# Four layers of gated attention: layer 2's norms and centred values placed inside layer 1's last steps, and its position products in a written TensorE order

## The chip, the cores and the metric

The kernel runs on one core of a Trainium2 chip. Its time is the device time of one execution in microseconds (us). A core has five engines with a queue of instructions each, which run side by side and wait for one another through semaphores: TensorE (PE in the profile, with PEld for its weight loads), VectorE (DVE), ScalarE (ACT), GpSimd (POOL) and SyncE (SP), which here only issues DMA transfers. TensorE's matrix products go into PSUM, eight banks of 128 by 512 floats; all else is in SBUF, 128 partitions wide.

## The reference

The input x has 16 blocks of 128 tokens by 128 features, and so has the context. Four layers each add two things to x, scaled by the tanh of a gate: a cross-attention on the context, and a feed-forward part, both on a normalised x. The change is at the seam between layer 1 and layer 2.

```python
# layer 1's feed-forward part: 8 components for each output feature, the one with the largest logit is taken
logits = (einsum('bsi,ki->bsk', x, sel_w) + sel_b).reshape(b, s, o, n)
probs = softmax(logits, axis=-1)
hard = one_hot(argmax(probs, axis=-1), n)
mask = stop_gradient(hard - probs) + probs
comp_outputs = einsum('bsi,noi->bsno', x, comp_w) + comp_b[None, None]
output = einsum('bsno,bson->bso', comp_outputs, mask)

# layer 2's attention: q = layernorm(x), k = v = ctx; 8 heads of 16 features
pos_emb = rpe[hops]                               # hops: 128 x 128 indices
ig, fg = gate_in @ igate_w.T + igate_b, gate_in @ fgate_w.T + fgate_b
csum = cumsum(log_sigmoid(fg))                    # with a zero ahead
log_D = csum_row - csum_col + ig, -inf above the diagonal
D = exp(log_D - max(log_D, axis=-1))
k_hop = einsum('bhvc,vmhc->bhvm', qh, pe)         # pe: pos_emb by heads
qk = einsum('bhsd,bhtd->bhst', qh, k / 4)
C = (qk + k_hop) * D
normalizer = maximum(abs(sum(C, axis=-1)), exp(-max_log_D))
h = C / (normalizer + 1e-6) @ vh
hn = layernorm over each head's 16 features, then * (1 + ln_w) + ln_b
```

## The kernel before, in words

All 16 blocks stay in SBUF. They are worked on in four chunks of four blocks (`NJ = 4`, `BJ = 4`, 512 tokens a chunk). `k.x` holds x, `k.xnT` the normalised x with the features on the partitions, `k.ctxT` the context in the same way, and `k.pe` the 128 by 128 position embeddings, gathered during the earlier layers.

**Who decides the order.** The program is written step by step, and a scheduler then puts the instructions of each engine into a fixed queue, by its own estimate of their times and by their dependencies. Where a part of the program sets `k.nc = Engines(...)` (line 47), each of four engines is wrapped in `InOrder` (line 28), which makes every instruction on it follow the one written before: there the written order is the queue's order, for all four engines. `Engines` is in force in layer 1's feed-forward part from line 936 to line 989, and not in layer 2's attention. The profile gives all instructions recorded through `InOrder` the line 38.

**Buffers.** `k.ps(...)` gives one of the PSUM banks. `w2k` is a pool of 13 tiles of 128 by 512, used for the exponentials `l1f_e`, the normalised `xn`, and layer 2's `l2_cm`. `l2_qz` has three buffers, so that queries are made two steps ahead of the products that use them. `l2_vx` lies in the buffer that `l1f_odd` had.

**Layer 1's feed-forward part** (`l1_ffn`, line 841) loops over steps `s`. Chunk `j` has eight components `c`, from 7 down to 0, at the steps 8j to 8j+7: TensorE computes its logits, ScalarE evicts them (`evicted`), VectorE keeps the running maximum `l1f_top` (`largest`). In the eight steps after that, for the same chunk, `less` subtracts the maximum on GpSimd (for the last chunk VectorE takes every odd component), `exped` takes the exponential on ScalarE, `outputs` is the product for the component, ScalarE adds its bias, `chosen` copies by predicate on VectorE, `paired` adds exponentials on GpSimd, and `summed` adds them up on TensorE. Then follow, in halves of 256 columns, `inverted` (the reciprocal into `l1f_r`, VectorE), `finished` (two VectorE operations, `l1f_r` and `l1f_y`), `output` (TensorE turns `l1f_y`) and `added` (VectorE adds it to x). Two tiles take turns for the shifted logits, `l1f_odd` and a part of `k.pe`, so the profile shows the last chunk's subtractions as `pe<-pe,l1f_top`. Chunk 3 finishes all eight pieces in one step, s = 35.

**Norms inside that loop.** `norms` (line 938) lists at which step the norm of which chunk begins. The first three entries are for this part itself, the last three are layer 2's first norm of chunks 0, 1 and 2. Each comes in three pieces, at the step listed, three steps later and five steps later: statistics on VectorE and a power of -1/2 on GpSimd (`ln_st`, `ln_mv`, `ln_rs`); the normalised `xn`, for layer 2's norms by GpSimd; four transposes on TensorE and a copy into `k.xnT`. That copy goes to ScalarE and VectorE in turn (`copy`, line 103). Chunk 3 is normed after the loop (line 990), with `xn` by VectorE.

**Layer 2's attention** (`l2_xattn`, line 1029). `centre` is the matrix that takes each head's mean off. `centred(j)` (line 1061) makes the values of four blocks: four products and a copy by ScalarE into `l2_vx`. `gates` (line 1074) is a generator that makes the gates: the products `l2_gw`, the logarithm of the sigmoid over many small VectorE operations down to `l2_lf`, a cumulative sum as a product (`l2_cs`), a transpose to `l2_gT`, a running maximum `l2_gm` (a scan), and a DMA of it to DRAM. `queries(n)` (line 1130) makes the masked queries of eight positions, four from the front (c = 0, VectorE) and four from the back (c = 1, GpSimd). `hops(n)` (line 1140) multiplies them with the position embeddings, eight products of 128 by 128, and ScalarE copies the results back over `k.pe` (line 1150). `last` does position 127, `biased` adds a bias to x on GpSimd (line 1165). Queries, hops and the steps of the gates alternate in one loop over 16 values of n:

```python
    for n in range(P // 8):
        if n + 2 < P // 8:
            ready[n + 2] = queries(n + 2)
        hops(n, ready.pop(n))
        next(chain, None)
        if n % 4 == 1:
            centred(n // 4)
        if n % 4 == 2:
            biased(n // 4)
```

After it a pipeline over pairs of blocks runs `decays` (line 1184: SyncE brings the maxima back from DRAM as `l2_cm`, GpSimd masks above the diagonal with `affine_select`, ScalarE takes four exponentials of 128 by 128 a tile, line 1203), `masked` (queries of two blocks, `l2_q`, GpSimd), `scores` (line 1216: products, the position scores added by VectorE or TensorE, multiplied with the decays), `values`, `turned`, `normed` (with a power on GpSimd, line 1269) and `added`. The scores need the whole of `k.pe` copied back.

Of the kernel before, what the change touches and what calls it, by code (L numbers as in the profile page):

```python
# [8 lines left out]
F32 = mybir.dt.float32  # L9
# [6 lines left out]
ALU = mybir.AluOpType  # L16
AX = mybir.AxisListType

P = 128
NB = 16  # L20
NJ = 4
BJ = NB // NJ
# [41 lines left out]
class Kernel:  # L64
# [32 lines left out]
    def sq(self, name, dtype=F32):  # L97
        return self.small.tile([P, P], dtype, tag="sq", name=name, bufs=14)
# [95 lines left out]
            except StopIteration as done:  # L194
                return done.value

    def norm(self, j, keep=None, twice=False, pow=None, by=None):

        nc = self.nc
        st = self.sm([P, BJ, 6], "ln_st")
        mv = self.sm([P, BJ, 2], "ln_mv")
        for i in range(BJ):
            nc.vector.bn_stats(st[:, i, :], self.x[:, BJ * j + i, :])
            nc.vector.bn_aggr(mv[:, i, :], st[:, i, :])
        rs = self.sm([P, BJ], "ln_rs")
        if pow is None:
            self.rsqrt(rs, mv[:, :, 1], 1e-5)
        else:  # L210
            nc.vector.tensor_scalar(rs, mv[:, :, 1], 1e-5, None, ALU.add)
            nc.gpsimd.tensor_tensor(rs, rs, pow, ALU.pow)
        yield
        xn = keep if keep is not None else self.w2k("xn").rearrange("p (b d) -> p b d", b=BJ)
        for i in range(BJ):
            (by or nc.vector).tensor_scalar(
                xn[:, i, :], self.x[:, BJ * j + i, :], mv[:, i, 0:1], rs[:, i : i + 1], ALU.subtract, ALU.mult
            )
        yield
        pt = self.ps("tr")  # L220
        for i in range(BJ):
            self.transpose(pt[:, i * P : (i + 1) * P], xn[:, i, :])
        if twice:
            nc.scalar.activation(self.chunk(self.xnT, j), pt, AF.Copy, scale=2.0)
        else:
            self.copy(self.chunk(self.xnT, j), pt)
        return xn

    def normed_rows(self, j, half):
# [48 lines left out]
def bc(ap, shape):  # L278
    return ap.to_broadcast(list(shape))
# [561 lines left out]
def l1_ffn(k):  # L841
# [4 lines left out]
    nc = k.nc  # L846
    C = 8
# [87 lines left out]

    k.nc = nc = Engines(k.tc, k.nc)

    norms = [(0, 1), (6, 2), (12, 3), (33, 0), (37, 1), (41, 2)]
    pieces = {}
    for first, j in norms:  # L940
        for at in (first, first + 3, first + 5):
# [1 line left out]
    under_way = {}  # L943
# [3 lines left out]
    for s in range(C * NJ + 24):  # L947
        j, c = s // C, C - 1 - s % C
# [35 lines left out]
            turn_positions(k, s // 2 + 6)  # L984
        for n in pieces.get(s, []):
            if n not in under_way:
                under_way[n] = k.norm(n[1], pow=k.half, by=nc.gpsimd if n[0] > C * NJ else None)
            next(under_way[n], None)
    k.nc = nc.nc
    k.layernorm(NJ - 1, pow=k.half)  # L990

# [32 lines left out]
    k.nc.scalar.activation(at.rearrange("p v d -> p (v d)"), pt[:, :width], AF.Copy, scale=4.0)  # L1026


def l2_xattn(k):


# [6 lines left out]
    nc = k.nc  # L1038
    H, DH, G = 8, 16, 4
# [6 lines left out]
    own = k.positions.tile([P, 2], F32, name="l2_own")  # L1046
    nc.vector.tensor_reduce(own, k.hm16x8.rearrange("p (g h) -> p h g", h=2), AX.X, ALU.add)
    nc.vector.tensor_scalar(own, own, 0.25, None, ALU.mult)

    centre = k.sq("l2_centre")  # L1050
    nc.vector.tensor_scalar(
        centre.rearrange("p (h d) -> p h d", h=H), bc(k.hm16x8.unsqueeze(2), [P, H, DH]), -1.0 / DH, None, ALU.mult
    )
    nc.vector.tensor_add(centre, centre, k.ident)


    vx = k.wts.tile([P, NB, H, 32], F32, tag="w16b", name="l2_vx")
    nc.gpsimd.memset(vx[:, :, :, DH:], 0.0)
    nc.gpsimd.memset(vx[:, :, :, DH : DH + 1], 1.0)

    def centred(j):
        pv = k.ps("acc")
        for i in range(BJ):
            k.mm(pv[:, i * P : (i + 1) * P], k.ctxT[:, BJ * j + i, :], centre)
        nc.scalar.copy(
            vx[:, BJ * j : BJ * (j + 1), :, 0:DH].rearrange("p b h d -> p (b h) d"),
            pv.rearrange("p (n d) -> p n d", d=DH),
        )

    sq = k.sq  # L1070
    g, low = sq("l2_g"), sq("l2_low")
    gm_d = k.dram.tile([P, P], F32, name="l2_gm_d")
# [1 line left out]
    def gates():  # L1074
# [24 lines left out]
        nc.vector.tensor_mul(u, u, e)  # L1099
        nc.vector.scalar_tensor_tensor(lf, lf, 0.0, u, ALU.min, ALU.subtract)  # L1100

        cs = sq("l2_cs")
        pc = k.ps("acc")[:, :P]
        k.mm(pc, k.tri, lf)
        yield
        nc.vector.tensor_copy(cs, pc)
        nc.vector.tensor_sub(g, ig, cs)
        pt = k.ps("tr")[:, :P]
        k.transpose(pt, g)
        yield  # L1110
# [1 line left out]
        nc.vector.tensor_copy(gT, pt)  # L1112
        nc.vector.tensor_tensor_scan(gm, gT, gT, -3e38, ALU.max, ALU.max)
        nc.sync.dma_start(out=gm_d, in_=gm)

        pt = k.ps("tr")[:, :P]
        k.transpose(pt, gm)
# [12 lines left out]
    def queries(n):  # L1130

        q = k.work.tile([P, 2, 4, H, NB], F32, tag="w4k", name="l2_qz", bufs=3)
        for c, v in enumerate((4 * n, 123 - 4 * n)):
            (nc.gpsimd if c else nc.vector).tensor_tensor(  # L1134
                q[:, c], bc(by_v[:, v : v + 4, :].unsqueeze(2), [P, 4, H, NB]),
                bc(quarter.unsqueeze(1).unsqueeze(3), [P, 4, H, NB]), ALU.mult,
            )
        return q
# [24 lines left out]
    def biased(j):  # L1163
        x = k.x[:, BJ * j : BJ * (j + 1), :]
        nc.gpsimd.tensor_tensor(x, x, bc(lnb.unsqueeze(1), [P, BJ, P]), ALU.add)

    chain = gates()
    ready = {0: queries(0), 1: queries(1)}
    for n in range(P // 8):
        if n + 2 < P // 8:  # L1170
            ready[n + 2] = queries(n + 2)
        hops(n, ready.pop(n))
        next(chain, None)
        if n % 4 == 1:
            centred(n // 4)
        if n % 4 == 2:
            biased(n // 4)
    last()
    next(chain, None)


    by_n = lambda t: t.rearrange("p (b h v) -> p (b h) v", b=2, h=2)
# [769 lines left out]
```

## Time and profile before

| | |
|---|---|
| median of 3 runs | 853.1 us (852.34 to 853.78) |
| profiled execution | 851.53 us |
| its span | 849.8 us |
| TensorE clock granted, mean | 0.919 |
| PE busy | 685.2 us, 81% of the span |
| PEld busy | 469.3 us, 55% |
| DVE busy | 520.3 us, 61% |
| ACT busy | 395.7 us, 47% |
| POOL busy | 452.2 us, 53% |

The span is from the first to the last recorded instruction; the profiled execution took 1.73 us more than its span. The names of the engines and of the views are the profile's. A row of a timeline gives the start and the length in us, the engine, the line, the operation, output and inputs with their shapes, how many instructions follow on one another (x4), and in brackets how long the engine was idle before and what released it. The length of such a group is from its first start to its last end. The chain of waits follows the work that ended last back from the end, at each step to what released it. Matmuls of floats come as two passes each, so 16 rows are eight products. Numbers behind tile names and digits in them are left out by the profile (`l_qz` is `l2_qz`).

### The profile page before, as it was taken

How to read it: one execution, taken by the hardware profiler on the slowest of the kernel's cores; microseconds unless marked ns; L12 is line 12 of the kernel's file. 1: busy time of each engine (PE TensorE's matmuls, PEld its weight loads, DVE VectorE, ACT ScalarE, POOL GpSimd, SP SyncE). 2: the span in 40 equal slices, each digit the busy share in tenths (PEclk: the TensorE clock that was granted, in tenths of full speed). 3: DMA queues.
4: the chain of work that ended last, by engine and by line, in shares of the span. 5: the costliest groups of instructions: out<-in, count | busy, mean ns of one | idle time of the engine just before them, and what ended most of it. 6: DMA issues, size and time to landing. Idle time of an engine off the chain costs nothing.

```text
span 849.8 us, 13272 instructions
## 1 busy us (share of the span) xinstructions
PE 685.2 (81%) x4321; PEld 469.3 (55%) x4321; DVE 520.3 (61%) x1463; ACT 395.7 (47%) x1001; POOL 452.2 (53%) x482
## 2 busy tenths in 40 slices
PE   3169993677897999899848798956999878999997
PEld 3159993343453555443328743434788765655556
DVE  5825553674645555788977456986411765777862
ACT  0025550442543455686505937511744355666552
POOL 5666656733744774686875916862200334555420
PEclk9999996787998999899959989875999999999999
DMA  8557773110000000000030405230000000000001
GB/s 262 133 172 212 207 175 91 49 35 10 20 13 20 23 24 23 3 0 1 2 98 20 146 1 161 77 124 15 11 1 0 1 2 1 1 0 1 1 7 43
DMA packets 43652, 46.47 MB, mean 55 GB/s; under 512 B 8368, under 2 KB 32560, under 8 KB 43456
## 3 DMA queue, kind: packets, MB, share of 16 engines
q1 hardware_dynamic: 37088, 35.63, 14.3%
q0 software_dynamic: 4384, 8.95, 4.3%
q10 hardware_dynamic: 2112, 1.05, 0.4%
q8 instruction: 34, 0.56, 0.3%
q14 instruction: 34, 0.28, 0.1%
HBM read 40.90 MB, written 4.72 MB: 54 GB/s over the span
## 4 chain that ended last, share of the span: by engine, by line
PE 50%; DVE 22%; issue 7%; POOL 7%; ACT 6%; DMA 3%; DVEq 0%; POOLq 0%; SPq 0%; ACTq 0%
PE ps_bank L112 21%; PE ps_bank L38 16%; PE ps_mm L112 4%; PE ps_acc L112 4%; DMA l_back<-l_out_d,l_rows 2%; ACT l_cm L1203 2%; DVE l_m L38 2%; DVE l1f_r L38 2%; PE ps_bank L116 1%; POOL l_ss L1269 1%; PE ps_mm L38 1%; DVE xn L38 1%; ACT pe L1150 1%; DVE xnT L38 1%; DVE l_up L38 1%
## 5 line engine op out<-in xcount | busy, mean ns | idle before, releaser
L1009 POOL DMA_INDIRECT pe<-in_L_xattn_rpe,itokT x65 | 64.6, 994 | 65.9 <-DVE l_top L739 20.9
L38 PE MATMUL ps_bank<-xnT,l1f_w 128*128 128x512 f32 x128 | 62.5, 618 | 0.4 <-ACT pe L38 0.4
L739 DVE TENSOR_REDUCE l_top<-ps_bank 128x8 f32<-128x512 f32 x64 | 39.8, 684 | 30.3 <-PE ps_bank L112 30.3
L486 DVE TENSOR_SCALAR l_h<-ps_mm,l_w 128x128 f32<-128x128 f32 x117 | 33.8, 345 | 35.4 <-ACT l_h L488 34.1
L771 ACT ACTIVATE l_a<-ps_bank 128x512 f32<-128x512 f32 x64 | 33.2, 602 | 45.8 <-PE ps_bank L112 45.7
L456 POOL DMA_INDIRECT l_xs<-l_rows_d,l_tok x39 | 37.0, 949 | 24.2 <-PE ps_acc L112 14.3
L112 PE MATMUL ps_acc<-l_w,l_h 128*128 128x128 f32 x312 | 45.5, 279 | 1.5 <-DVE l_y L498 1.3
L1203 ACT ACTIVATE l_cm<-l_cm,l_g 128x128 f32<-128x128 f32 x128 | 40.2, 404 | 13.9 <-POOL l_cm L1196 13.9
L112 PE MATMUL ps_mm<-l_xT,l_w 128*128 128x128 f32 x312 | 44.2, 279 | 0.4 <-ACT l_xT L471 0.4
L112 PEld LDWEIGHTS ps_acc<-l_w,l_h 128*128 128x128 f32 x312 | 40.0, 193 | 2.4 <-ACT l_h L488 2.3
L38 POOL TENSOR_TENSOR l2f_o<-l2f_o,l2f_sc 128x264 f32<-128x264 f32 x10 | 7.7, 779 | 61.7 <-PE ps_bank L38 59.6
L112 PEld LDWEIGHTS ps_mm<-l_xT,l_w 128*128 128x128 f32 x312 | 39.8, 196 | 0.6 <-ACT l_xT L471 0.6
L112 PE MATMUL ps_bank<-l_qz,pe 128*128 128x128 f32 x256 | 34.2, 293 | 6.8 <-POOL l_qz L1134 4.8
L1440 ACT ACTIVATE l2f_h<-ps_bank,sb_L_ffn_b1T 128x264 f32<-128x264 f32 x64 | 27.7, 483 | 24.3 <-PE ps_bank L112 24.3
L1449 DVE TENSOR_SCALAR l2f_y<-ps_bank,sb_L_ffn_b2T 128x264 f32<-128x264 f32 x16 | 7.9, 493 | 50.2 <-PE ps_bank L112 50.2
L38 POOL DMA_INDIRECT l_back<-l_out_d,l_rows x32 | 30.8, 961 | 13.3 <-issue 5.8
L38 PEld LDWEIGHTS ps_bank<-xnT,l1f_w 128*128 128x128 f32 x128 | 24.1, 200 | 24.9 <-issue 17.3
L112 PEld LDWEIGHTS ps_bank<-l_qz,pe 128*128 128x128 f32 x256 | 32.6, 208 | 7.8 <-POOL l_qz L1134 5.6
L38 PE MATMUL ps_bank<-xnT,sb_L_xattn_gru_whT 128*128 128x512 f32 x72 | 35.8, 606 | 0.0
L38 POOL TENSOR_TENSOR ln_rs<-ln_rs,neg_half 128x4 f32<-128x4 f32 x14 | 14.7, 1052 | 36.9 <-DVE ln_rs L38 35.9
L1134 POOL TENSOR_TENSOR l_qz<-xnT,l_quarter 128x512 f32<-128x512 f32 x16 | 29.3, 1843 | 8.6 <-DVE l_d L1095 3.8
L38 PE MATMUL ps_bank<-l_upT,sb_L_xattn_gru_wiT 128*128 128x512 f32 x72 | 32.9, 593 | 0.0
(425 smaller groups left out, 1980.7 us busy)
## 6 DMA issues: line engine op xcount, KB each, us to landing
l_w<-in_L_xattn_w1b SPq DMA_DIRECT2D x39, 258.0 KB
l_cm<-l_gm_d SPq DMA_DIRECT2D x64, 128.0 KB
l_out_d<-l_y SPq DMA_DIRECT2D x39, 64.0 KB
sb_L_xattn_W<-in_L_xattn_W SPq DMA_DIRECT2D x1, 2048.0 KB
sb_L_ffn_w<-in_L_ffn_w SPq DMA_DIRECT2D x1, 2048.0 KB
pe<-in_L_xattn_rpe,itokT POOLq DMA_INDIRECT x65, 2.6
x<-in_x ACTq DMA_DIRECT2D x4, 256.0 KB
ctxT<-in_ctxT SPq DMA_DIRECT2D x1, 1024.0 KB
```

The lines of the kernel that those rows point to most:

```text
L38: done = op(*args, **kw)
L112: self.nc.tensor.matmul(out, lhsT, rhs, start=start, stop=stop)
L116: self.nc.tensor.transpose(out, in_, self.ident[:n, :n])
L456: nc.gpsimd.indirect_dma_start(out=xs, out_offset=None, in_=rows_d, in_offset=bass.IndirectOffsetOnAxis(ap=tok[:, n : n + 1].bitcast(U32), ...
L486: nc.vector.tensor_scalar(h[:, cols], ph[:, cols], bias, 0.0, ALU.add, ALU.max)
L739: done = nc.vector.tensor_reduce(top[:, 32 * g : 32 * g + 8], ss[g].rearrange("p (n s) -> p n s", n=8), AX.X, ALU.max)
L771: nc.scalar.activation(a, ss[g], AF.Exp, scale=scale)
L1009: dma = nc.gpsimd.indirect_dma_start(out=k.pe[:, g if g < G - 1 else P - 1, :], out_offset=None, in_=k.a["L2_xattn_rpe"], in_offset=bass.I ...
L1134: (nc.gpsimd if c else nc.vector).tensor_tensor(q[:, c], bc(by_v[:, v : v + 4, :].unsqueeze(2), [P, 4, H, NB]), bc(quarter.unsqueeze(1).un ...
L1150: nc.scalar.copy(k.pe[:, v : v + 4, :].rearrange("p v q -> p (v q)"), ph)
L1203: nc.scalar.activation(part, part, AF.Exp, scale=-1.0, bias=g[:, n : n + 1])
L1440: nc.scalar.activation(h, ph, AF.Gelu, bias=b1[:, e * NF + f : e * NF + f + 1])
```

## The change

Four things change.

1. Layer 2's norms of chunks 0 and 1 begin at the steps 27 and 34 of layer 1's loop where they began at 33 and 37; chunk 2's stays at 41. The copies into `k.xnT` of all four chunks of layer 2's first norm are ScalarE's.
2. The centring matrix, the memsets of `l2_vx` and the four times four products with their copies leave `l2_xattn`. They become a generator, `l2_values`, which is created at step 38 of layer 1's loop and advanced at each step from 44 on. There the order of all four engines is as written.
3. The loop over gates, queries and hops runs with TensorE's order as written; the other engines are left to the scheduler. The generator of the gates has three more stops, so that its steps fall between later hops.
4. From n = 8 on both halves of the queries are made by VectorE.

```diff
-    def norm(self, j, keep=None, twice=False, pow=None, by=None):
+    def norm(self, j, keep=None, twice=False, pow=None, by=None, copy=None):
...
-            self.copy(self.chunk(self.xnT, j), pt)
+            (copy or self.copy)(self.chunk(self.xnT, j), pt)
...
-    norms = [(0, 1), (6, 2), (12, 3), (33, 0), (37, 1), (41, 2)]
+    norms = [(0, 1), (6, 2), (12, 3), (27, 0), (34, 1), (41, 2)]
...
-                under_way[n] = k.norm(n[1], pow=k.half, by=nc.gpsimd if n[0] > C * NJ else None)
+                second = n[0] > 2 * C
+                under_way[n] = k.norm(
+                    n[1], pow=k.half, by=nc.gpsimd if second else None, copy=nc.scalar.copy if second else None
+                )
             next(under_way[n], None)
+
+        if s == C * NJ + 6:
+            k.l2_values = l2_values(k)
+        if s > C * NJ + 11:
+            next(k.l2_values, None)
     k.nc = nc.nc
-    k.layernorm(NJ - 1, pow=k.half)
+    k.layernorm(NJ - 1, pow=k.half, copy=k.nc.scalar.copy)
...
+def l2_values(k):
+    nc = k.nc
+    H, DH = 8, 16
+    k.l2_vx = vx = k.wts.tile([P, NB, H, 32], F32, tag="w16b", name="l2_vx")
+    nc.gpsimd.memset(vx[:, :, :, DH:], 0.0)
+    nc.gpsimd.memset(vx[:, :, :, DH : DH + 1], 1.0)
+    centre = k.sq("l2_centre")
+    nc.vector.tensor_scalar(
+        centre.rearrange("p (h d) -> p h d", h=H), bc(k.hm16x8.unsqueeze(2), [P, H, DH]), -1.0 / DH, None, ALU.mult
+    )
+    nc.vector.tensor_add(centre, centre, k.ident)
+    for j in range(NJ):
+        yield
+        pv = k.ps("acc")
+        for i in range(BJ):
+            k.mm(pv[:, i * P : (i + 1) * P], k.ctxT[:, BJ * j + i, :], centre)
+        nc.scalar.copy(
+            vx[:, BJ * j : BJ * (j + 1), :, 0:DH].rearrange("p b h d -> p (b h) d"),
+            pv.rearrange("p (n d) -> p n d", d=DH),
+        )
...
 # l2_xattn: the same lines are taken out here, with centred(j); instead
+    vx = k.l2_vx
...
 # gates: three more stops
         nc.vector.scalar_tensor_tensor(lf, lf, 0.0, u, ALU.min, ALU.subtract)
+        yield
         cs = sq("l2_cs")
...
         nc.vector.tensor_sub(g, ig, cs)
+        yield
         pt = k.ps("tr")[:, :P]
...
         nc.sync.dma_start(out=gm_d, in_=gm)
+        yield
...
 # queries
-            (nc.gpsimd if c else nc.vector).tensor_tensor(
+            (nc.gpsimd if c and n < P // 16 else nc.vector).tensor_tensor(
...
+    told = Engines(k.tc, nc)
+    told.vector, told.scalar, told.gpsimd = nc.vector, nc.scalar, nc.gpsimd
+    k.nc = told
     chain = gates()
...
         hops(n, ready.pop(n))
         next(chain, None)
-        if n % 4 == 1:
-            centred(n // 4)
         if n % 4 == 2:
             biased(n // 4)
     last()
-    next(chain, None)
+    for _ in chain:
+        pass
+    k.nc = nc
```

On the engines' queues this gives the following. VectorE: chunk 0's statistics stand right behind the running maximum of chunk 3's component 4; chunk 1's stand where chunk 0's stood, chunk 2's where they were; the two operations for the centring matrix stand among chunk 3's last statistics; between `l2_lf` and the scan there are five queries where there were two. GpSimd: chunk 0's power stands ahead of the last four index subtractions of chunk 2, and its `xn` ahead of the last one; the masked queries `l_q` of the first blocks and chunk 1's power stand ahead of chunk 3's subtraction for component 4; the memsets stand behind chunk 2's `xn`. TensorE: four centred products stand behind chunk 3's last turned output, the other twelve between the transposes of chunk 2's and chunk 3's `xn`. ScalarE: 18 copies of position products stand ahead of the first exponential of the decays where 12 stood, and 46 exponentials ahead of the last such copy where 52 stood. SyncE's queue keeps its order.

More of the change, by code (lines that the diff above doesn't have):

```diff
@@ L1048, in l2_xattn @@
     nc.vector.tensor_scalar(own, own, 0.25, None, ALU.mult)
[L1050 to L1068, printed above, removed]
+    vx = k.l2_vx
     sq = k.sq
```

## The prediction

> **What bounds the kernel now.** I read the engines' shares, the chain of waits from 380 us to 620 us, the timelines of VectorE, GpSimd (POOL), TensorE and ScalarE between 390 and 515 us, and the windows. No engine fills the span (TensorE 81%), so the change is worth what it does to the chain where it acts: the end of layer 1 and the start of layer 2. Starts below are on the clock of before. The chain (start, length, work):
>
> ```profile
> 464.76 3.31 DMA l_cm<-l_gm_d
> 468.20 1.03 POOL l_cm L1196
> ...
> 473.81 2.15 ACT l_cm L1203 x7
> ...
> 477.10 2.17 ACT l_cm L1203 x7
> ...
> 494.81 0.48 ACT pe L1150
> 495.33 17.65 PE ps_bank L112 x96
> ```
>
> From the DMA of the gate maxima on, the chain stays on ScalarE, exponentials (L1203) and copies of position products (L1150) in turn, until the last copy ends at 495.28; only then do the scores start. The windows (PE, PEld, DVE, ACT, POOL busy with counts, granted clock) confirm it:
>
> ```profile
> 440.00:442.00 2.00, 0.55 (x3) 0.18 (x1) 1.33 (x3) 0.00 (x0) 1.84 (x2) 0.50 0.00 0
> 480.00:484.00 4.00, 2.22 (x19) 1.91 (x17) 1.55 (x2) 4.00 (x13) 4.00 (x6) 1.00 0.01 2
> ```
>
> The first shows TensorE at half clock just before layer 2, the second ScalarE without a gap and VectorE mostly idle. TensorE's waits for GpSimd's queries (up to 1.78 us) are real but not what ends last: its position products are over at 491.4. In layer 1's last 30 us VectorE is the bound (29.11 busy of 30 from 396):
>
> ```profile
> 426.08 0.17 DVE L38 TENSOR_SCALAR ln_rs<-ln_mv 128x4 f32<-128x4 f32 x1
> 428.18 0.69 DVE L38 COPY xnT<-ps_bank 128x512 f32<-128x512 f32 x1 [1.93 <-PE ps_bank L38]
> 428.78 1.75 DVE L38 RECIPROCAL l1f_r<-ps_bank 128x256 f32<-128x256 f32 x1
> ...
> 441.38 6.91 DVE L1134 TENSOR_TENSOR l_qz<-xnT,l_quarter 128x512 f32<-128x512 f32 x4
> ...
> 457.62 1.03 DVE L1134 TENSOR_TENSOR l_qz<-xnT,l_quarter 128x512 f32<-128x512 f32 x1
> ```
>
> It waits 1.93 us for a norm's transposes, copies, and only then goes on to the last reciprocals. GpSimd and TensorE beside it:
>
> ```profile
> 405.18 1.27 POOL L38 TENSOR_TENSOR pe<-pe,l1f_top 128x512 f32<-128x512 f32 x1 [5.02 <-DVE l1f_top L38]
> ...
> 411.25 1.47 POOL L38 TENSOR_TENSOR pe<-pe,l1f_top 128x512 f32<-128x512 f32 x1
> ...
> 441.43 8.02 POOL L1134 TENSOR_TENSOR l_qz<-xnT,l_quarter 128x512 f32<-128x512 f32 x4
> ...
> 485.66 0.63 POOL L1196 TENSOR_SCALAR_AFFINE_SELECT l_cm<-l_cm 128x512 f32<-128x512 f32 x1
> 486.26 1.33 POOL L1134 TENSOR_TENSOR l_qz<-xnT,l_quarter 128x512 f32<-128x512 f32 x1
> ```
>
> ```profile
> 442.54 3.56 PE L112 MATMUL ps_bank<-l_qz,pe 128*128 128x128 f32 x16 [1.99 <-DVE l_qz L1134]
> ...
> 458.15 1.95 PE L112 MATMUL ps_bank<-l_qz,pe 128*128 128x128 f32 x16
> ```
>
> Sixteen passes are eight products: 0.445 us each cold, 0.24 warm.
>
> **Step A: layer 1's tail, to the complete xnT (441.28 before).** The norms' copies go to ScalarE, which idles 13.52 us there: VectorE loses the stall and the copy, −1.93 −0.60. Chunk 0's statistics (407.91 to 409.70, 1.79) move to about 393.9, where VectorE's gaps of 0.76 and 0.37 take part of them; they cost some 0.5 there: −1.25. Chunk 1's move into their old place. Against this stands GpSimd. Its pow for chunk 0 now comes before the last four index subtractions and waits from 392.8 to the statistics' end at 395.6 (2.8), then pow 1.03 and chunk 0's xn 3.15: 7.0 us into an idle of 5.02, so it is 2.0 late, free at 410.1 instead of 408.1. Queued ahead of the subtraction for component 4 (411.25 before) are now layer 2's masks (2.32) and chunk 1's pow (1.14): with 1.47 for itself it ends at 415.0, ScalarE's exponential and bias add 1.2, and VectorE, there at 414.4, stalls until 416.2: +1.8 (0 if GpSimd keeps up; 2.8 if the wait for the statistics is longer). The last exponential stands behind a norm's copy on ScalarE: +1.0. The operation at 416.28 runs without GpSimd's norm beside it, 0.42 (row of 420.74) for 1.08: −0.66. So the reciprocals come 1.6 sooner; the two centre operations cost +0.6, and the operation at 433.33 (1.50) falls to 0.43: chunk 3's last statistics end 2.1 sooner, at 435.7, with the centre ready about 435.3.
>
> The memsets of the values (1.81 and 0.33) cost nothing: GpSimd is now done with chunk 1 early, so chunk 2's pow can start with its statistics at 427.1 (426.25, 0.9 later by the terms so far), and 1.02 + 3.24 + 2.14 and a bias addition of 1.26 end at 434.8, before the pow of chunk 3 is called for at 435.7. Without that 0.9 of cover all of the lateness falls on chunk 3's norm, 2.1 at most. SyncE's queue keeps its order.
>
> Then comes TensorE, whose written order puts 16 centred products before chunk 3's transposes. It starts cold: 4×0.445 = 1.8, chunk 2's transposes 1.06; the run of 442.54 came back to full clock after 3.1 us, so the other twelve go near warm, 12×0.26 = 3.1; chunk 3's transposes 0.9 and ScalarE's copy with its start 0.8. From 435.3 that is 443.0: **+1.7**. All cold (12×0.445, transposes 1.25) gives 445.4, +4.1; warm and without the GpSimd stall about −2. I take the middle because the clock's own row lies inside the stretch.
>
> **Step B: xnT to the gate maxima (441.28 to 462.70).** TensorE is warm now, so the first eight products take 1.95 for 3.56: −1.6. But VectorE's fixed run between lf and the scan's end grows from 5.0 (one query ahead of cs, one ahead of the scan) to queries 1.2, 1.2, cs and g 0.6, 1.4, two of 1.03 for step 8, gT 0.28, scan 1.20 and 0.3 of waits, 8.2: +3.2. Net **+1.6** (0 if the queries fit into waits, +3.2 if the clock stays low). The maxima land at 466.0; the path to the first exponential (DMA out, DMA in, mask) is unchanged at 6.6, so it starts at 472.55.
>
> **Step C: ScalarE's stretch.** Before, from 469.25 to 495.28: 52 exponentials, 20 position copies, 2 value copies and one small copy. In the changed order 6 exponentials stand after the last position copy, 6 more position copies before the first exponential, and the value copies are in layer 1's idle ScalarE: 6×0.30 + 6×0.475 + 2×0.50 = **−5.65**, 20.4 for 26.0, end 492.95.
>
> The cover: after the maxima VectorE makes 13 queries until the one that ScalarE's last run needs, plus 0.64 of small work. That run (copies 0.475 twice, the small copy 0.3, 12 exponentials 3.6) and the products' 0.98 must follow, so it has until 487.1, 21.1 us: ScalarE stays the bound up to 1.57 us a query. Alone a query takes 1.03, beside GpSimd's queries 1.73 (6.91/4). GpSimd now has thirteen affine selects of 0.61 there and no query, so I take some 1.2, nearer the lone row; the ends 1.03 and 2.0 (rows of 462.62 and 476.97) go to the rivals.
>
> The page "SBUF — State Buffer" of the Trainium skill, section "SBUF: two separate sides", speaks against the change: the port pair that VectorE and GpSimd share is held for a whole instruction, so a two-input VectorE operation would wait out each affine select. The row is milder: four queries on each finish in 8.02 where taking turns would need 4×1.03 + 4×1.33 = 9.44. By the rule thirteen selects add 7.9 to thirteen queries, VectorE is 0.9 late, and the forecast would be 851.7; by the row it is unchanged.
>
> **Step D: after 495.** The scores begin with another order of exponentials and masks behind them. VectorE is nearly full there (56.00 busy of 62 from 518) and waits for GpSimd's pow by 0.53 to 2.59 us. I know no sign: 0, bounds ±1.5.
>
> Sum: 1.7 + 1.6 − 5.65 = −2.35. Profiled execution 851.53 (span 849.8 and 1.73 around it) gives 849.2; the median lies 1.57 above that execution: **850.8**.
>
> **Rivals.** *VectorE takes over in the late queries (slower).* At 2.0 a query, as in its two slowest rows, the needed one is ready at 492.6, 5.5 late: −2.35 + 5.5 = +3.2, 856.3. It makes the kernel slower from 1.75 us a query. For it: TensorE's waits show that late queries matter, and VectorE gets sixteen where it had eight; against it: GpSimd's load halves. *The norms come too early and TensorE stays cold.* Step A's upper end costs 2.4 more: 853.1, no change. For it: clock 0.50 for 17 us. *The tail gains too.* GpSimd keeps up (−1.8), no wait behind the copy (−1.0), transposes warm (−0.5): −5.6, 847.5. For it: GpSimd's 5.02 idle.
>
> **How the numbers follow.** Forecast 0.42, VectorE 0.25, cold 0.15, tail 0.18. No change means within 1.7 us (0.2%), about what a measurement of this kernel can tell. The forecast's own range, 848.5 to 853, lies mostly below 851.4: I count 0.32 of it as faster, 0.10 as same. Faster 0.32 + 0.18 = 0.50, same 0.10 + 0.15 = 0.25, slower 0.25. The range takes the tail case's centre and VectorE's: 847.5 to 856.3, leaving out half of each, about 0.2.
>
> **What would show it.** In the trace after: no VectorE wait before an xnT copy near 428 (A right); a VectorE wait for ScalarE at a predicated copy near 415 (GpSimd late); xnT complete near 443 and the scan's end near 466; first exponential near 472.5; last position copy near 493, with ScalarE full before it. ScalarE idle behind TensorE, and that behind VectorE's queries at over 1.6 us, would prove the slower rival. A scan that ends before 463 would make the gain larger than the range.

## The result, and the profile after

The changed kernel takes 862.01 us (median of 4 runs, 858.96 to 868.41) where the kernel before takes 852.72 (852.16 to 853.78) beside it: ratio 1.0125, 95% interval 1.0085 to 1.0165. The ratios and intervals here and below are those on record, worked out from the fast runs of both kernels; they need not equal the quotients of the medians. It is slower by 9.3 us, and the forecast of 850.8 us with its range up to 856.3 was wrong. The profiled execution took 863.66 us (span 862.0, granted clock 0.917).

Six marks of the two traces say where the time went. All are read from the timelines; the fifth is the start of the transposes.

| mark | before | after | difference |
|---|---|---|---|
| chunk 3's `xnT` complete | 441.28 | 444.86 | +3.58 |
| scan of the maxima ends | 462.70 | 467.62 | +4.92 |
| first exponential of the decays | 469.25 | 474.32 | +5.07 |
| last copy of position products ends | 495.28 | 494.84 | −0.44 |
| last transposes of the feed-forward norm begin | 585.87 | 595.48 | +9.61 |
| end of the span | 849.8 | 862.0 | +12.2 |

Up to the last copy the change gains 0.44 us of the 2.35 that were forecast. Then, in 90 us of score pipeline in which no line of the program was touched, the kernel loses 10.05 us, and another 2.6 after it.

The windows of the changed kernel that answer to the two shown of before (PE, PEld, DVE, ACT, POOL busy with counts, granted clock, DMA share, GB/s):

```profile
440.00:442.00 2.00, 2.00 (x11) 2.00 (x11) 0.00 (x0) 0.74 (x2) 1.09 (x1) 0.50 0.00 0
480.00:484.00 4.00, 3.21 (x26) 2.83 (x25) 4.00 (x4) 4.00 (x12) 4.00 (x4) 1.00 0.86 258
```

TensorE is still at half clock at 440, but busy now; the full clock is granted from 442.01 to 452.25. In the second window ScalarE is full, as before, and so are VectorE and GpSimd: step C's cover is in use, and it holds.

TensorE around the seam (timeline):

```profile
437.17 2.08 PE L38 MATMUL ps_bank<-l_centre,ctxT 128*128 128x128 f32 x8 [1.69 <-DVE l_centre L38]
439.04 1.06 PE L38 MATMUL ps_bank<-ident,xn 128*128 128x128 f32 x4
439.90 3.85 PE L38 MATMUL ps_bank<-l_centre,ctxT 128*128 128x128 f32 x24
443.58 0.60 PE L116 MATMUL ps_bank<-ident,xn 128*128 128x128 f32 x4
```

The twelve centred products of the third row stand ahead of chunk 3's transposes (fourth row) and take 3.85 us; chunk 3's `xn` was ready at 439.73.

Now the score pipeline, VectorE's rows of one pair of blocks. In the kernel before, the denominators of the next pair (L1262 to L1268) go on through the end of this pair, the add into x (L1279):

```profile
525.45 0.42 DVE L1274 TENSOR_TENSOR l_t<-ps_bank,l_ss 128x256 f32<-128x256 f32 x1 [1.83 <-POOL l_ss L1269]
525.79 0.16 DVE L1262 TENSOR_SCALAR l_den<-ps_bank 128x16 f32<-128x16 f32 x1
526.20 0.16 DVE L1263 TENSOR_TENSOR l_den<-l_den,ps_bank 128x16 f32<-128x16 f32 x1
526.72 0.83 DVE L1279 TENSOR_TENSOR x<-x,l_t 128x256 f32<-128x256 f32 x1 [0.36 <-POOL l_t L1278]
...
541.64 0.16 DVE L1262 TENSOR_SCALAR l_den<-ps_bank 128x16 f32<-128x16 f32 x1
...
545.69 0.59 DVE L216 TENSOR_SCALAR l2f_xn<-x,ln_mv,ln_rs 128x128 f32<-128x128 f32 x2
```

The feed-forward norm of layer 2 (`l2f_xn`, last row) comes only after the fourth pair's denominators. In the changed kernel (19 is added to the line numbers of `l2_xattn`) the same instructions stand in another order:

```profile
524.99 0.43 DVE L1293 TENSOR_TENSOR l_t<-ps_bank,l_ss 128x256 f32<-128x256 f32 x1 [1.83 <-POOL l_ss L1288]
526.26 0.84 DVE L1298 TENSOR_TENSOR x<-x,l_t 128x256 f32<-128x256 f32 x1 [0.85 <-POOL l_t L1297]
527.13 0.49 DVE L205 BATCH_NORM_STATS2 ln_st<-x 128x6 f32<-128x128 f32 x2
527.53 0.16 DVE L1281 TENSOR_SCALAR l_den<-ps_bank 128x16 f32<-128x16 f32 x1
...
535.31 0.42 DVE L1298 TENSOR_TENSOR x<-x,l_t 128x256 f32<-128x256 f32 x1 [1.41 <-POOL l_t L1297]
...
537.80 1.81 DVE L216 TENSOR_SCALAR l2f_xn<-x,ln_mv,ln_rs 128x128 f32<-128x128 f32 x3 [0.44 <-POOL ln_rs L212]
539.54 0.62 DVE L1284 TENSOR_SCALAR l_den<-l_den 128x16 f32<-128x16 f32 x1
```

Here VectorE first waits for GpSimd's weights of the head norm (`l_t`, 0.85 and 1.41 us), adds into x, takes the statistics, and only then begins the next pair's denominators. Of the third pair's, the norm of layer 2's feed-forward part (`l2f_xn`) even stands in the middle, and waits for GpSimd's power. GpSimd in turn waits for those denominators, for its next power (timeline, GpSimd, changed kernel):

```profile
529.94 2.90 POOL L1288 TENSOR_TENSOR l_ss<-l_ss,neg_half 128x16 f32<-128x16 f32 x1 [1.77 <-DVE l_ss L1287]
542.22 2.90 POOL L1288 TENSOR_TENSOR l_ss<-l_ss,neg_half 128x16 f32<-128x16 f32 x1 [2.10 <-DVE l_ss L1287]
549.93 2.90 POOL L1288 TENSOR_TENSOR l_ss<-l_ss,neg_half 128x16 f32<-128x16 f32 x1 [1.62 <-DVE l_ss L1287]
561.32 2.90 POOL L1288 TENSOR_TENSOR l_ss<-l_ss,neg_half 128x16 f32<-128x16 f32 x1 [3.96 <-DVE l_ss L1287]
```

So the two engines take turns. From the first of the eight powers to the last are 58.2 us after (522.04 to 580.23) and 49.4 before (522.50 to 571.88): 8.8 of the 10.05 us. The seven intervals do not grow alike: that between the second and the third power, where the norm stands in the middle, goes from 6.48 to 12.28 us, that between the fifth and the sixth from 4.52 to 7.39, while the first shrinks from 9.04 to 7.90. The views of the waits from 520 to 600 us sum it (engine and what it waited for: us in all, times, longest), before and after:

```profile
POOL l_ss L1269 <- DVE l_ss L1268: 5.9, 4, 3.5
```

```profile
POOL l_ss L1288 <- DVE l_ss L1287: 9.7, 5, 4.0
DVE x L1298 <- POOL l_t L1297: 3.8, 5, 1.4
```

The last of these waits is 0.4 us in the kernel before.

### The profile page after: what moved, and what is told of

It reads as the page before. It is cut to its first block, busy times and chain, and to the rows that moved or that the text cites. A ratio compares the mean times of both kernels' runs of the same rounds, so it can differ in the third digit from the quotient of the medians.

```text
span 862.0 us, 13270 instructions
## 1 busy us (share of the span) xinstructions
PE 693.1 (80%) x4321; PEld 476.5 (55%) x4321; DVE 528.2 (61%) x1469; ACT 396.2 (46%) x1003; POOL 443.6 (51%) x474
## 4 chain that ended last, share of the span: by engine, by line
PE 49%; DVE 19%; POOL 9%; issue 7%; DMA 5%; ACT 4%; SPq 0%; ACTq 0%; POOLq 0%; DVEq 0%
PE ps_bank L112 21%; PE ps_bank L38 17%; PE ps_mm L112 4%; PE ps_acc L112 4%; PE ps_bank L116 2%; DMA l_back<-l_out_d,l_rows 2%; DVE l_m L38 2%; POOL l1f_odd L38 2%; DMA l_cm<-l_gm_d 2%; DVE xn L38 1%; PE ps_mm L38 1%; DVE l1f_r L38 1%; POOL l_ss L1288 1%; DVE l_up L38 1%; DVE xnT L38 1%
## 5 line engine op out<-in xcount | busy, mean ns | idle before, releaser
L38 PE MATMUL ps_bank<-xnT,l1f_w 128*128 128x512 f32 x128 | 60.0, 595 | 0.6 <-ACT pe L38 0.4
L1215 POOL TENSOR_SCALAR_AFFINE_SELECT l_cm<-l_cm 128x512 f32<-128x512 f32 x32 | 26.2, 845 | 20.2 <-DMA l_cm<-l_gm_d 19.2
L1150 DVE TENSOR_TENSOR l_qz<-xnT,l_quarter 128x512 f32<-128x512 f32 x24 | 29.9, 1302 | 5.9 <-ACT xnT L226 5.2
```

The lines of the kernel that those rows point to most:

```text
L38: done = op(*args, **kw)
L1150: (nc.gpsimd if c and n < P // 16 else nc.vector).tensor_tensor(q[:, c], bc(by_v[:, v : v + 4, :].unsqueeze(2), [P, 4, H, NB]), bc(quarter ...
L1215: nc.gpsimd.affine_select(out=by_n(cm), in_=by_n(cm), pattern=[[0, 4], [1, P]], compare_op=ALU.is_ge, fill=1e30, base=0, channel_multiplie ...
```

## The experiments

The theory is that the scheduler, given another program upstream, put the score pipeline into another order, and that this order costs the time. The rivals are that an edit costs it directly (TensorE's order, the queries, the norms), through buffers that come free or transfers that start at another time. "Order" below is the order of VectorE's queue from the first decays to layer 2's feed-forward part, the other engines' with it unless one is named. Where an order was held, it was by ordering edges between neighbours in a queue, which add no semaphore:

```diff
+    for engine, order in QUEUES.items():      # the other kernel's order
+        mine = [instructions of this engine, in the order of the program]
+        for a, b in zip(order, order[1:]):
+            order_after(mine[b], mine[a])     # scheduling only, no wait
```

The runs lie on three chips, on which the kernel before takes 852.6, 880.4 and 877.9 us (runs 1 to 4, 5 to 8, 9 to 12). The chip of the result's two traces is not on record; their times are those of the first, and they are put with it. Each ratio is to the kernel before on the same chip; traces of one chip are compared with one another, or by lengths within a trace. Two such lengths matter: from the running maximum of layer 1's last chunk to the last copy of position products (up to the copies), and from there to the start of the last transposes of the feed-forward norm (scores). The running maximum is counted from the start of its first operation, 386.92 in the kernel before.

| run | order | up to the copies | scores | ratio (95%) |
|---|---|---|---|---|
| before | before's | 108.4 | 90.6 | 1 |
| changed | new | 107.9 | 100.6 | 1.0125 (1.0085–1.0165) |
| 1 changed, order held | before's | 107.4 | 91.7 | 1.0016 (0.9983–1.0048) |
| 2 before, order held | changed's | 108.0 | 100.5 | 1.0139 (1.0091–1.0187) |
| 3 no early norms | before's | 109.0 | 90.6 | 0.9988 (0.9956–1.0021) |
| 4 TensorE order and queries | before's, held | 112.0 | 90.1 | 1.0020 (0.9993–1.0047) |
| 5 values split | before's | 106.8 | 90.9 | 0.9969 (0.9943–0.9994) |
| 6 changed, VectorE held | before's on VectorE | 113.0 | 91.0 | 1.0027 (0.9997–1.0057) |
| 7 split, fewer queries | before's | 109.3 | 91.1 | 0.9953 (0.9933–0.9974) |
| 8 early norms alone | before's | 114.5 | 93.6 | 1.0047 (1.0021–1.0073) |
| 9 TensorE order alone | a third one | 113.0 | 89.9 | 0.9990 (0.9969–1.0012) |
| 10 split, fewer stops | before's | 107.4 | 91.2 | 0.9967 (0.9947–0.9987) |
| 11 the same, fewer queries | before's | 108.8 | 89.8 | 0.9961 (0.9941–0.9982) |
| 12 changed, pairs apart | a fourth one | 113.1 | 92.5 | 1.0020 (1.0001–1.0039) |

**Runs 1 and 2: the two orders exchanged.** Run 1 is the changed kernel with the order of before held on all engines; run 2 is the kernel before with the order of the changed one.

> The changed kernel, with the queues of the score pipeline (decays to the first gather of layer 2's feed-forward part) held to the order that they have in the kernel before, by ordering edges alone; up to the scores it is the changed kernel. Theory 1 (the loss is in the queue order behind 495 us): the last position copy stays near 494.8, the last norm's transposes come back from 590.0 to about 580, the profiled execution is 850 to 852.5 and the ratio to before 0.997 to 1.002. Theory 2 (the loss is what the front leaves behind: clock, buffers, DMAs): still 858 to 864, ratio over 1.006.

> The kernel before, with the score pipeline's queues held to the order that they have in the changed kernel; up to the scores it is the kernel before. Theory 1: last position copy at 495.3 as before, last norm's transposes near 590, 860 to 866 us, ratio 1.009 to 1.016. Theory 2: 852 to 854, ratio within 1.002.

Measured: 853.25 and 863.65 us. The time goes with the order and not with the edits. Before's program with the new order loses the whole amount, and the changed program without it is not measurably slower than the kernel before. Run 2's trace has the same waits of GpSimd for `l_ss` as the changed kernel's, 1.76, 2.10, 1.63 and 3.96 us.

**Run 3: the change without its norms.**

```diff
-    norms = [(0, 1), (6, 2), (12, 3), (27, 0), (34, 1), (41, 2)]
+    norms = [(0, 1), (6, 2), (12, 3), (33, 0), (37, 1), (41, 2)]   # and the copies in turn, as before
```

> The changed kernel with layer 2's norms and their copies back as before (steps 33, 37, 41, copies in turn); values, TensorE order and queries as changed. Its score pipeline's queues come out nearly as in the kernel before without any help. Theory 1: 851 to 853.5, last position copy at 494 to 496, since the earlier norms brought nothing (last reciprocals at 429.05 against 428.78). Theory 2, or if the early norms were worth the 1.6 us that I gave them: 1.6 us or more behind the changed kernel's own place at every mark up to 495, and 858 or more in all.

Measured: 851.9 us. With the norms in their old place the scheduler gives the pipeline before's order by itself, and the loss is gone with no edge set. Chunk 3's `xnT` is complete 57.94 us after the running maximum, against 57.92 in the changed kernel: the early norms bring the seam nothing.

**Run 4: TensorE's order and the queries alone**, on the kernel before, order held.

> Only the written TensorE order and the late queries by VectorE; norms and values as before, and the score pipeline's queues held to the order of the kernel before. Without the sixteen products ahead of chunk 3's transposes xnT should be complete at 441.3 as before (444.9 in the changed kernel), the scan end near 464, the first exponential near 470.7, and ScalarE's stretch 21.5 us (20.5 and the two value copies): last position copy near 492.2, 849 to 851.5 us, ratio 0.995 to 0.999. If the order of TensorE itself costs what it brings: ratio 1.000 or more.

Measured: 853.87 us, ratio 1.0020: the forecast gain (0.995 to 0.999) did not come, and the rival's 1.000 or more did. The scan comes later than in any run above, 27.3 us after `xnT` where before has 21.4 and the changed kernel 22.8. TensorE's product for the gates shows why (timelines of run 4, then of the changed kernel):

```profile
443.49 6.85 PE L38 MATMUL ps_bank<-l_gw,xnT 128*128 128x16 f32 x32
```

```profile
448.10 3.64 PE L38 MATMUL ps_bank<-l_gw,xnT 128*128 128x16 f32 x32
```

Without centred products in front, TensorE does these products and its first position products at a granted clock of 0.50, which lasts from 425.65 to 452.96, although TensorE is busy without a gap from 439.95 on. The other traces agree as to the centred products: in the nine that have them in front (changed, 1, 3, 5 to 7, 10 to 12) the half clock around the seam lasts 10.2 to 13.7 us, in the five that have not (before, 2, 4, 8, 9) 17.1 to 30.7. So the centred products cost time ahead of `xnT` and earn some of it back: the clock comes up sooner. They are not all of it: the kernel before has none in front either, and its half clock ends 3.2 us after its position products begin (442.54 to 445.77), where run 4's lasts 13.0. Why it lasts so long there no run shows.

**Run 5: half of the centred products behind the transposes**, with the norms of before. Of the sixteen, eight stay ahead of chunk 3's transposes.

```diff
-        if s > C * NJ + 11:
+        if C * NJ + 11 < s <= C * NJ + 11 + 3:
             next(k.l2_values, None)
...
     k.layernorm(NJ - 1, pow=k.half)
+    for _ in k.l2_values:      # in TensorE's written order
+        pass
```

> As the run without the early norms, but only eight of the sixteen centred products stand ahead of chunk 3's transposes; the other eight stand behind them, in the wait for the first query. The score pipeline's queues come out as in the kernel before. If the sixteen products delayed xnT (444.9 for 441.3) and also brought TensorE's clock back for the gates, both are to be had: marks counted from the running maximum at 391.5, xnT at +50 (before +49.8, without the early norms +53.4), the scan's end at +72 (+71.3 and +75.4), the last position copy at +99 (+103.8 and +104.5): 847 to 850.5 us, ratio 0.993 to 0.998. Rival: eight products are too little, the clock stays at half into the gates as in the run with only the TensorE order and the queries: scan's end at +75, last copy at +105, ratio 1.000 to 1.003.

Measured: 876.51 us, faster than before by 0.1 to 0.6%. `xnT` is complete 55.62 us after the running maximum (57.94 in run 3), and the copies end 2.2 us sooner than there. The expectation counts from a later operation of the running maximum, at 391.45 in the kernel before; counted so, `xnT` is at +51.1 for the forecast +50, the scan's end at +75.0 for +72, the last copy at +102.3 for +99. The ratio came as forecast, the marks did not: the scan ends where the rival had it, though not for the rival's reason, since the products for the gates run at full clock (3.64 us at 470.67).

**Run 6: the changed kernel, VectorE's order alone held.**

> The changed kernel with only VectorE's queue in the score pipeline held to the order of the kernel before; the scheduler orders the other engines around it. If VectorE's order alone carries the loss: power for blocks 4 and 5 back from 542.2 to about 538.0, last norm's transposes near 586 to 587, 851 to 854 us, ratio 0.998 to 1.003. If GpSimd's or TensorE's order carries it: 857 to 863.

Measured: 883.06 us, with the scores back at 91.0. VectorE's queue carries the loss: GpSimd's order, left to the scheduler, is still unlike before's, and the loss is gone. Counted from the running maximum, the copies end 6.2 us later than in run 5, and 4.2 of these have arisen at the last reciprocals, ahead of the gates; run 8 shows them too (see the last section).

**Run 7: run 5 with VectorE making both halves of the queries from n = 12 on only.**

> As the split values, but VectorE takes both halves of the queries only from n = 12 on, so it makes one query less between lf and the scan. If the queries ahead of the scan cost their own time: scan's end 1.0 us sooner than with the split alone, and the last copy 0.5 to 1 sooner, ratio about 0.001 better. If GpSimd's queries are late beside its affine selects (2.0 us each): TensorE waits for GpSimd again, last copy up to 1.5 later than with the split alone, ratio about 0.001 worse.

Measured: 877.54 us, ratio 0.9953. It is faster than both kernels; its interval overlaps that of run 5, so the queries' own share is not settled. Its trace does not show the forecast gain: the scan ends 0.7 us later than in run 5, where 1.0 sooner was expected, and the last copy 2.5 later.

**Run 8: the early norms and ScalarE's copies alone**, on the kernel before.

> The kernel before with only the early norms and their copies by ScalarE; queues of the score pipeline as before. By my sum the last reciprocals come 1.6 us sooner (427.2 for 428.8) and with them xnT, 849.5 to 852, ratio 0.997 to 0.999. By the trace of the changed kernel GpSimd's masks and power ahead of a subtraction eat it: VectorE waits about 1.1 us twice near 415 to 418, reciprocals at 429, 852 to 854, ratio within 0.002 of 1.

Measured: 885.32 us, slower by 0.2 to 0.7%, outside both ranges of the expectation. The last reciprocals come 45.93 us after the running maximum, where run 5 on the same chip has 41.73 (see the last section). The scores take 93.6 us here although the order is before's; no run explains these 3 us, and they show how far one trace can lie from the others with the order unchanged.

**Run 9: TensorE's order alone**, nothing held.

> The kernel before with only TensorE's fixed order in the position products and the three more stops in the gates; queries, norms and centred values as before. No queue is held to an order here, and the scheduler gives the score pipeline another order on VectorE and GpSimd than before's, though nothing of the pipeline is touched. Theory 1 (the cost of the change is the scheduler's new order): 1.5 us for the fixed TensorE order, as the fourth run had it with the order of before held, plus a part or the whole of the 11 us that the order of the changed kernel costs: 857 to 866 where the kernel before takes 852.6, ratio 1.005 to 1.016, with the last layer-2-FFN transposes over 466 us after the reciprocals. Theory 2 (only the one order of the changed kernel is bad): 854, ratio 1.002.

Measured: 876.5 us, as before. The first theory was too broad: this order of VectorE's queue is new in many places and costs nothing. In its trace the next pair's denominators begin at 551.8 and the add into x comes at 553.9, so the pairs overlap as in the kernel before. It is not a changed order that costs, but this one.

**Runs 10 and 11: runs 5 and 7 with fewer stops in the gates.** The middle one of the three stops is taken out, the one ahead of the transposes of the gates; the other two stay (the expectation speaks of one, but the last comes after the scan and holds up no gate).

> The fifth run's kernel (half of the centred products behind the last transposes, old norms) with one more stop in the gates instead of three: the one ahead of the cumulative gates' product stays, the two behind it go. Every queue of the score pipeline comes out as before. If the stops that stand between scan and gates are worth their hops (each lets TensorE do 6 to 7 us of position products, and VectorE's scan waits for that only where the gate's small matmul stands behind them), the scan ends 1 to 2 us sooner than in the fifth run: ratio 0.994 to 0.996. Rival (the end of the position copies is set by VectorE's queries and ScalarE's copies alone by now): 0.997, as the fifth run.

> The run above with VectorE making both halves of a query from the twelfth group on alone, not from the eighth. In the seventh run that was worth 0.0016 of the time. Theory: the same here, ratio 0.992 to 0.995. Rival (both gains are the same idle time of VectorE, so that they do not add): 0.995 to 0.997.

Measured: ratios 0.9967 and 0.9961. The scan ends 77.5 us after the running maximum in both, 2.0 sooner than in run 5, and the last copy ends no sooner (107.4 against 106.8): the rival of run 10 holds, and run 11's ratio lies in its rival's range. Runs 5, 7, 10 and 11 cannot be told apart from one another.

**Run 12: the changed kernel with the pairs made to overlap.** Seven edges on VectorE: the add into x of each pair stands behind the next pair's sum of denominators. All else is the scheduler's.

```diff
+        if u + 1 < NB // 2:
+            order_after(add_into_x, next_pair_l_ss)   # scheduling only, no wait
```

> The changed kernel with seven ordering edges: on VectorE, the add into x of each pair of blocks stands behind the next pair's sum of denominators. The rest of the order is the scheduler's, and it is still unlike before's. Theory 1 (the overlap of one pair's last step with the next pair's first ones carries the cost): most of the 11 us comes back, 852 to 856, ratio 0.999 to 1.004. Theory 2 (it is the feed-forward norm that stands ahead of the next denominators, or GpSimd's order): 860 to 866, ratio 1.008 to 1.016.

Measured: 880.39 us, ratio 1.002. The scores take 92.5 us where the changed kernel's trace has 100.6, though much of the order is still unlike before's. One pair in its trace, with the denominators' last step ahead of the add:

```profile
553.28 0.42 DVE L1293 TENSOR_TENSOR l_t<-ps_bank,l_ss 128x256 f32<-128x256 f32 x1 [2.25 <-POOL l_ss L1288]
...
555.77 0.17 DVE L1287 SCALAR_TENSOR_TENSOR l_ss<-l_ss,l_den 128x16 f32<-128x16 f32 x1
555.86 0.42 DVE L1298 TENSOR_TENSOR x<-x,l_t 128x256 f32<-128x256 f32 x1
```

The add no longer waits for GpSimd. From the first power to the last it is 50.7 us (550.34 to 601.02) where the changed kernel has 58.2. Seven edges bring back some 8 of the 10 us, so the place of the add is the greater part of the loss. How much of that is the add's own wait is not settled: the feed-forward norm needs the added x, so the edges also move it out of the middle of the third pair's denominators (in this trace it comes at 570.75, behind them and still ahead of the fourth pair's).

## Why the prediction was wrong

**Step D failed.** It said "I know no sign: 0, bounds ±1.5", and it measured +10.05 us up to the last transposes. It named the right place, a VectorE that is nearly full and waits for GpSimd's powers, but took only ScalarE's order of exponentials and masks to be different, and set bounds as if the waits could change a little. Runs 1, 2 and 12 show what stood there instead: the scheduler's order decides whether the last step of one pair and the first of the next lie beside each other, and without that the seven intervals between the powers grow by 8.8 us together, 5.8 of them in one. No step of the sum contained VectorE's order in that stage; the list of queue changes ahead of the prediction ends at the last copy of position products. The other 2.6 us after the last transposes are not explained: in the other traces that length varies from 262.7 to 267.3 us, those of the changed kernel and of runs 6 and 7 being the long ones.

**Step A was mis-sized: +3.58 for +1.7.** Its second half was right. From chunk 3's last statistics to `xnT` it had 435.7 to 443.0, 7.3 us, and the trace has 437.48 to 444.86, 7.4. What failed is "the reciprocals come 1.6 sooner": they come at 429.05 for 428.78, 0.27 later (timeline, VectorE, changed kernel):

```profile
412.80 1.00 DVE L38 TENSOR_TENSOR pe<-pe,l1f_top 128x512 f32<-128x512 f32 x1
414.88 0.70 DVE L38 COPY_PREDICATED ps_bank<-pe,ps_bank 128x512 f32<-128x512 uint32 x1 [1.08 <-ACT ps_bank L38]
...
418.37 0.70 DVE L38 COPY_PREDICATED ps_bank<-pe,ps_bank 128x512 f32<-128x512 uint32 x1 [1.13 <-POOL pe L38]
...
429.05 1.75 DVE L38 RECIPROCAL l1f_r<-ps_bank 128x256 f32<-128x256 f32 x1
```

The stalls were about as costed, 1.08, 1.13 and 0.71 us (at 426.65) where 1.8 and 1.0 were taken. But VectorE's single operations beside GpSimd's took longer than the rows that priced them, for example 1.25 for 0.88 and 1.00 for 0.68; five such rows (at 406.83, 408.99, 411.39, 412.80 and 422.58) come to 1.7 us more, most of the 1.9 that are missing. No term of the sum held this. In the second half the twelve centred products took 3.85 us for 3.1, and the transposes and the copy behind them made up for it. Run 3 confirms that the early norms gain nothing.

**Step B: +1.34 for +1.6**, and the way from the maxima to the first exponential 6.70 for 6.6. The second is right. The first is near its number in part by luck, since both of its terms were too large and their errors cancel: from `xnT` to the end of `l_lf` it is 0.8 us shorter where 1.6 was taken, and from there to the scan's end 2.2 longer (7.18 for 5.0) where 3.2 was taken. The scan alone fell from 1.20 to 0.42 us.

**Step C: right.** ScalarE's stretch is 20.52 us for 20.4 predicted. The late queries and the affine selects (timelines, VectorE and GpSimd, changed kernel):

```profile
471.84 12.25 DVE L1150 TENSOR_TENSOR l_qz<-xnT,l_quarter 128x512 f32<-128x512 f32 x10
```

```profile
472.77 14.12 POOL L1215 TENSOR_SCALAR_AFFINE_SELECT l_cm<-l_cm 128x512 f32<-128x512 f32 x13 [7.61 <-DMA l_cm<-l_gm_d]
```

Ten queries took 1.2 us each, as taken. From the third on one query and one select begin every 1.28 us, less than the 1.03 + 0.61 = 1.64 of their lone rows one after the other; the last four selects, with no query beside them, took 0.63 each. So the slower rival, in which VectorE takes over in the late queries, did not happen; the kernel came out slower as it forecast, but for another reason. That of the cold TensorE happened in part (half clock until 442), inside the +3.58; the tail's gain did not happen.

**The sum** of A to C was −2.35 and measured −0.44; nearly all of the difference is step A's. Without step D the change would have been worth nothing that can be measured, which is what run 1 shows.

## What to carry to other kernels

Where a scheduler orders the queues, an edit can change the order of stages that it does not touch, and that may cost more than the edit can gain. So the queues are compared to the end of the program, and above all in every stage where two engines feed each other: there one looks for whether the last step of one round and the first of the next still overlap. If they do not, a few ordering edges at that seam may do: here seven brought back some 8 of 10 us. And work moved into a gap of TensorE had two sides here: in front of the critical transposes it costs its length, but the clock comes up sooner for what follows. Splitting it (run 5) gave back 2.3 us at `xnT` and kept the half clock at 10.2 us, though its gates still took longer than in the kernel before (23.9 us from `xnT` to the scan's end for 21.4).

## What the runs showed of the hardware

VectorE can lose far more to GpSimd than one instruction. The same subtraction that took 1.25 us in the changed kernel's trace, and 0.68 where it is alone, took 5.51 in run 6 on the second chip (5.50 in run 8, and 5.53 in run 12 on the third chip). VectorE, then GpSimd, in run 6:

```profile
431.39 0.48 DVE L38 SCALAR_TENSOR_TENSOR x<-ps_bank,l1f_minus,x 128x256 f32<-128x256 f32 x1 [1.60 <-PE ps_bank L38]
...
432.39 5.51 DVE L38 TENSOR_TENSOR pe<-pe,l1f_top 128x512 f32<-128x512 f32 x1
```

```profile
431.35 1.26 POOL L1181 TENSOR_TENSOR x<-x,sb_L_xattn_ln_b 128x512 f32<-128x512 f32 x1
432.58 1.26 POOL L38 TENSOR_TENSOR pe<-pe,l1f_top 128x512 f32<-128x512 f32 x1
433.81 1.25 POOL L38 TENSOR_TENSOR l1f_e<-l1f_e 128x512 f32<-128x512 f32 x1
435.03 2.31 POOL L1231 TENSOR_TENSOR l_q<-xnT,l_own 128x256 f32<-128x256 f32 x4
```

Behind the instruction under way GpSimd runs six more back to back at their usual length, and VectorE's ends 0.56 us after GpSimd's last. In run 5, with the old norms, the same row takes 0.87, and the reciprocals come 4.2 us sooner. The section "SBUF: two separate sides" of the page "SBUF — State Buffer" of the Trainium skill has the shared port pair go to whichever starts first, for the whole instruction. By that rule VectorE would have waited out the instruction under way, 0.22 us more; it waited out seven. The changed kernel's own trace fits the rule here: its row (1.25 us from 406.83) ends 0.56 us after the GpSimd instruction that was under way (ended at 407.52), and GpSimd's next two are stretched instead, the first to 1.72 us, the second as follows:

```profile
409.17 1.71 POOL L38 TENSOR_TENSOR pe<-pe,l1f_top 128x512 f32<-128x512 f32 x1
```

The early norms, which put GpSimd's work back to back there, so cost 0.3 us at the reciprocals in two traces (the changed kernel and run 1) and 4 us in three. These differ in the chip, but not in the chip alone. In runs 6, 8 and 12 the granted clock is 0.50 for 3.4 us just before (427.57 to 430.98 in run 6), and TensorE's products there take longer; the five other traces of these chips, with the old norms, have the full clock at that place. Run 6, then the changed kernel, where the clock is full:

```profile
429.24 1.90 PE L38 MATMUL ps_bank<-l1f_e,ident 128*128 128x512 f32 x2
```

```profile
404.55 1.02 PE L38 MATMUL ps_bank<-l1f_e,ident 128*128 128x512 f32 x2
```

So the turned output comes late, VectorE waits 1.60 us for it, and its subtraction starts 21.59 us after the running maximum where the changed kernel has 19.89, beside other instructions of GpSimd. Whether the moment of the start or the chip decides is not shown.
